# An LSTM step on ScalarE and the reload of output rows: waits, queues and a planner's table

## The chip, the cores and the metric

The kernel runs on one core of one Trainium2 chip. Its engines are TensorE (matrix products; its weight loads are listed apart), VectorE, ScalarE, GpSimd and SyncE, which issues transfers. Time is microseconds on the device. The core takes instructions of each engine in a fixed order; engines wait for each other through semaphores.

## The reference, cut to what matters

A two-layer network: images become tokens (a convolution and an attention), text tokens are joined, layer 0 is a windowed attention and a mixture of eight experts, layer 1 a phasor attention and then an LSTM over 569 time steps of 16 sequences with 256 units. The change lies in the LSTM and in what follows it:

```python
x_proj = jnp.einsum('btd,gd->btg', x, W_ih) + b_ih + b_hh
def step(carry, xp):
    h, c = carry
    gates = xp + h @ W_hh.T
    i, f, g, o = jnp.split(gates, 4, axis=-1)
    c = jax.nn.sigmoid(f) * c + jax.nn.sigmoid(i) * jnp.tanh(g)
    h = jax.nn.sigmoid(o) * jnp.tanh(c)
    return ((h, c), h)
...
inc = jnp.cumsum(w, axis=1)          # w: hidden states that a linear layer selects
prefix = inc - w
suffix = inc[:, -1:, :] - inc
return 2.0 * lstm_out + prefix * fw_att + suffix * bw_att
```

The suffix needs the sum over all steps, so no output row is final before the last step.

## The kernel before, in words

The first half of the time goes to the tokens, the attention of layer 0 and the experts. From about 1,723 us on, two things run side by side: the LSTM's 569 steps, a chain in which each step needs the one before, and the layers' work on later time steps (layer 1's attention and the projections `x_proj`, the functions `fronts` and `backs`), called the other streams here.

*Time blocks.* The steps are cut into ten blocks (`BLOCKS`: 32 steps, eight times 64, 25), a block into units of 8 steps (`STEPS`). The projections of a block are added up by VectorE into `xp` (L1591) and stored to HBM in `XCD` (input, forget and cell gates) and `XOD` (output gate) by SyncE's queue (L1596, L1600). For each unit `load` (L1672) brings them back into `XC` and `XO`, two buffers each, as soon as the block's `backs` are done. So the first step of a block can't begin before the other streams have finished that block.

*A step* (`steps`, L1664). Two PSUM banks hold the sums: `GC` (96 columns, three gates) and `GO` (64 columns, output gate). ScalarE copies the step's input into them (`begin`, L1691, and `begin_out`, L1696), TensorE adds the recurrent products (L1734, L1743), ScalarE reads the sums through tanh (L1754, L1760), and TensorE clears the banks with products with zeros (`clear`, L1684) so that they can be begun again for the next step. VectorE makes the cell state (L1766, L1772) and turns it (L1779), ScalarE takes its tanh (`th`, two buffers in turn, L1787), VectorE turns the output gate (L1792) and writes the hidden state `X` (L1794). Then the next step's recurrent products begin.

*The planner.* The order of each engine's instructions is not left to a scheduler: `Order` lists the pieces of the chain and of the other streams on a clock of its own and puts them down one by one. For the chain it reads the table `STEP` (L129): for every piece the engine, how long that engine is taken, when the result is there, after which piece it comes and with what hop between them. A piece of another stream is put in where it ends before the chain will need its engine, by that table, with a small allowance (`plan.spare`, set at L1713). When the chain can't go on, because a block is not projected yet, the other streams get the engines to themselves until it can. On the chip each engine then works in exactly that order: an instruction that stands ahead of the chain's next one is done first.

*Dependences and waits.* The framework derives the waits from what each instruction reads and writes, those between two instructions of the same engine too. An instruction holds one wait itself; further ones are put into separate semaphore instructions in front of it, on the same engine's queue. A wait for a later instruction of an engine stands for all earlier ones, and the framework leaves out what it thus knows already.

*The output rows.* `sums_of` (L1801) makes the running sums for each run of 16 steps. There is no room for all output rows while the other streams use the memory, so finished ones go to HBM (`PD`, L1868). When the other streams are done, their memory becomes `O` (L1902), the rows are loaded back into it by SyncE's queue in pieces of eight units, 1 MB each (L1905), and later rows are written to it directly. After the last step the suffix is added to `O` and it is stored (L1934, L1938).

Of the kernel before, what the change touches and what calls it, by code (L numbers as in the profile page):

```python
# [12 lines left out]
AF = mybir.ActivationFunctionType  # L13
# [72 lines left out]
def time_of_rows():  # L86
# [44 lines left out]
    "out hidden": ("PE", 0.24, 0.42, "hidden", -0.17),  # L131
    "gates": ("ACT", 0.16, 0.26, "hidden", 0.065),
    "clear": ("PE", 0.06, 0.25, "gates", 0.06),
    "out gate": ("ACT", 0.12, 0.22, "out hidden", 0.065),
    "input": ("ACT", 0.14, 0.24, "clear", 0.065),
    "products": ("DVE+", 0.22, 0.22, "gates", 0.035),
    "cell": ("DVE+", 0.19, 0.19, "products", 0.035),
    "cell turned": ("DVE", 0.13, 0.21, "cell", 0.035),
    "out clear": ("PE", 0.06, 0.25, "out gate", 0.06),
    "tangent": ("ACT", 0.14, 0.23, "cell turned", 0.095),  # L140
    "out input": ("ACT", 0.12, 0.22, "out clear", 0.065),
    "out gate turned": ("DVE", 0.15, 0.23, "out gate", 0.035),
    "state": ("DVE+", 0.18, 0.18, "tangent", 0.035),
}
# [150 lines left out]
def kernel(ctx: ExitStack, tc: tile.TileContext, a: dict, out: bass.AP):  # L295
    nc = tc.nc
# [56 lines left out]
    before = route.tile([128, E, E], F32, name="before")  # L353
    strict = route.tile([128, 128], F32, name="strict")
    ones = route.tile([128, 128], F32, name="ones")
    between = route.tile([128, 1], F32, name="between")
# [18 lines left out]
    first = Order()  # L375
# [1288 lines left out]
    def steps():  # L1664

        act = ls.tile([128, 4 * 32], F32, name="act_init", tag="act", bufs=3)
        nc.vector.memset(act[:, 96:], 0.0)
        before, begun, loaded = None, set(), set()  # L1670

        def load(k):  # L1672
            j, u, n = UNITS_ALL[k]
            loaded.add(k)
            nc.sync.dma_start(
                XC[k % 2][:, :n, :], XCD[j][:, :, u : u + n, :].rearrange("a b t x -> (a b) t x")
            )
            for q in range(4):
                nc.sync.dma_start(XO[k % 2][32 * q + NB : 32 * q + 32, :n, :], XOD[j][q, :, u : u + n, :])
            plan.mark(("loaded", k), 4.0)  # L1680

        def clear(g, n, last):
            for q in range(4):
                nc.tensor.matmul(  # L1684
                    g[32 * q : 32 * q + 32, :n], nil[:, :32], nil[:, :n], start=True, stop=last
                )

        def begin(k, t):
            begun.add((k, t))
            yield "input"  # L1690
            nc.scalar.copy(GC[:, :96], XC[k % 2][:, t, :])  # L1691

        def begin_out(k, t):
            begun.add((k, t, "out"))
            yield "out input"
            nc.scalar.copy(GO[:, :64], XO[k % 2][:, t, :])  # L1696

        def ready(k):

            n = 2 * UNITS_ALL[k][0]  # L1700
            return [("back", n + i, slot) for i in range(2) for slot in range(2)]

        for k, (j, u, n) in enumerate(UNITS_ALL):
            if k not in loaded:
                for event in ready(k):
                    yield "at", event
                load(k)
            yield "at", ("loaded", k)

            after = [("back", 2 * (j + 1) + i, slot) for i in range(2) for slot in range(2)]  # L1710
            done = sum(plan.past(e) for e in after) if j + 1 < len(BLOCKS) else 4
            ahead = plan.past(("back", 2 * j + 3, 0))
            plan.spare = 0.0 if ahead else 0.2 if done >= 4.0 * u / BLOCKS[j][1] - AHEAD else 0.45  # L1713
            if (j, u) in run_of:
                r = run_of[j, u]
                if r >= 4:
                    yield "at", ("sums", r - 4)
                hidden[r] = XS_OF[r % 4][:, :, : RUNS[r][2], :]
            X = hidden[r][:, :, u - RUNS[r][1] :, :]
            for t in range(n):  # L1720
                at, last = f"{k}_{t}", (k, t) == (len(UNITS_ALL) - 1, n - 1)
                if before is None:
                    yield "hidden"
                    clear(GC, 96, True)
                    clear(GO, 64, True)
                if (k, t) not in begun:
                    yield from begin(k, t)
                    yield from begin_out(k, t)
                yield "hidden"
                for kk in range(2 if before is not None else 0):  # L1730
                    for half in range(2):
                        for q in range(4):
                            own = 512 * (q // 2) + 96 * (2 * (q % 2) + half)
                            nc.tensor.matmul(  # L1734
                                GC[32 * q : 32 * q + NB * (1 + half), :96],
                                before[:, kk, NB * (1 - half) :], Whh[:, kk, own : own + 96],
                                start=False, stop=(kk + half == 2),
                            )
                yield "out hidden"
                for kk in range(2 if before is not None else 0):  # L1740
                    for q in range(4):
                        own = 512 * (q // 2) + 384 + 64 * (q % 2)
                        nc.tensor.matmul(  # L1743
                            GO[32 * q : 32 * q + 32, :64], before[:, kk, :],
                            Whh[:, kk, own : own + 64], start=False, stop=(kk == 1),
                        )
                if (
                    k + 1 < len(UNITS_ALL) and k + 1 not in loaded
                    and all(plan.past(e) for e in ready(k + 1))
                ):  # L1750
                    load(k + 1)
                nxt = (k, t + 1) if t + 1 < n else (k + 1, 0)
                yield "gates"
                nc.scalar.activation(act[:, :96], GC[:, :96], AF.Tanh, scale=0.5)  # L1754
                if not last:
                    yield "clear"
                    clear(GC, 96, False)
                to = ls.tile([128, 64], F32, name=f"to{at}", tag="to", bufs=3)
                yield "out gate"
                nc.scalar.activation(to, GO[:, :64], AF.Tanh, scale=0.5)  # L1760
                ahead = nxt[0] in loaded and plan.past(("loaded", nxt[0]))
                if ahead:
                    yield from begin(*nxt)
                ab = ls.tile([128, 2, 32], F32, name=f"ab{at}", tag="ab", bufs=2)
                yield "products"
                nc.vector.scalar_tensor_tensor(  # L1766
                    ab, act[:, :64].rearrange("p (g x) -> p g x", g=2), 1.0,
                    act[:, 64:].rearrange("p (g x) -> p g x", g=2), ALU.add, ALU.mult,
                )
                act = ls.tile([128, 4 * 32], F32, name=f"act{at}", tag="act", bufs=3)  # L1770
                yield "cell"
                nc.vector.scalar_tensor_tensor(  # L1772
                    act[:, 96:], ab[:, 1, :], 0.5, ab[:, 0, :], ALU.mult, ALU.add
                )

                cT = ls.tile([128, 2 * NB], F32, name=f"cT{at}", tag="cT", bufs=2)
                yield "cell turned"
                nc.vector.transpose(cT, act[:, 96:])  # L1779
                if not last:  # L1780
                    yield "out clear"
                    if j >= len(BLOCKS) - 2:
                        product(GO[:, :D], ident, Whh[:, 0, :D], start=True, stop=True)
                    clear(GO, 64, False)
                th = ls.tile([128, 2, NB], F32, name=f"th{at}", tag="th", bufs=2)
                yield "tangent"
                nc.scalar.activation(th.rearrange("p k x -> p (k x)"), cT, AF.Tanh, scale=0.5)  # L1787
                if ahead:
                    yield from begin_out(*nxt)
                toT = ls.tile([128, 2, 2 * NB], F32, name=f"toT{at}", tag="toT", bufs=2)  # L1790
                yield "out gate turned"
                nc.vector.transpose(toT.rearrange("p k x -> p (k x)"), to)  # L1792
                yield "state"
                nc.vector.scalar_tensor_tensor(  # L1794
                    X[:, :, t, NB:], toT[:, :, NB:], 1.0, th, ALU.add, ALU.mult
                )
                before = X[:, :, t, :]
            if u + n == RUNS[r][1] + RUNS[r][2]:
                plan.mark(("steps", r))

# [85 lines left out]
    with tc.manual_schedule(engines=ENGINES):  # L1886
# [13 lines left out]
        bg.close()  # L1900
        op = ctx.enter_context(tc.tile_pool(name="out", bufs=1))
        tail["O"] = op.tile([128, sum(map(len, UNITS_OF)), D], F32, name="O")  # L1902
        for u in range(0, tail["stored"], 8):
            u1 = min(u + 8, tail["stored"])
            nc.sync.dma_start(tail["O"][:, u:u1, :], PD[:, u:u1, :])  # L1905
        plan.run([chain, rest])
    route.release()

# [153 lines left out]
```

## Time and profile before

| | us |
|---|---|
| median of 5 runs | 3381.17 (3378.01 to 3384.28) |
| the profiled execution, its own time | 3380.79 |
| its span, first to last instruction | 3378.9 |
| tokens, attention, experts: up to the first step | 1,723 |
| the 569 steps | 1,723 to 3,338.6 |
| of them with other streams' work beside | 1,723 to about 3,167 |
| suffix and stores after the last step | 3,338.6 to 3,378.9 |

Busy time of the engines in three stretches, from the profile's view by windows:

| window, us | TensorE | VectorE | ScalarE | GpSimd |
|---|---|---|---|---|
| 2400 to 2600 | 192.93 | 147.14 | 111.76 | 21.65 |
| 3200 to 3300 | 80.28 | 52.12 | 45.16 | 0.00 |
| 3300 to 3379 | 33.77 | 46.45 | 18.03 | 0.00 |

How to read the profile. A time line row has the start, the time taken, the engine (PE is TensorE, PEld its weight loads, DVE VectorE, ACT ScalarE, SP SyncE; a q behind it means that the engine's queue works and not the engine), the line, the operation, what it writes and reads, and in brackets how long the engine had been idle and what ended that. The chain of work lists start, duration and piece. A view of one line gives the number of its instructions, their shortest, median and longest duration in ns, and the first and last start. Ends of products on TensorE are modelled.

### The profile page before, as it was taken

The page shows a single profiled execution, that of the slowest core. Times are in us where ns is not written, and L with a number is a line of the kernel's source. Part 1 is how long each engine was busy: PE and PEld are TensorE (multiplying, and loading weights), DVE is VectorE, ACT ScalarE, POOL GpSimd, SP SyncE. Part 2 cuts the span into 40 slices and gives each one's busy share as a digit, 9 for nine tenths or more (in the row PEclk, how much of TensorE's full clock was granted, in tenths as well). Part 3 has the DMA queues.
Part 4 walks back from the last instruction along what each step waited for, and adds up shares of the span by engine and source line. Part 5 has one row for each costly group of instructions (what it writes and reads, how often), then busy time and mean ns, then how long its engine had stood idle before and what let it go on. Part 6 is the DMA issues. An engine that isn't in the chain of part 4 may idle for free.

```text
span 3378.9 us, 135926 instructions
## 1 busy us (share of the span) xinstructions
PE 3069.7 (91%) x57536; PEld 2228.4 (66%) x57536; DVE 2016.0 (60%) x6785; ACT 1483.0 (44%) x5032; POOL 789.7 (23%) x1524
## 2 busy tenths in 40 slices
PE   6999989999859999997899999999999999999884
PEld 3666666666648888886565666666666666666553
DVE  4677777766732222222565777777777777776555
ACT  3545545454412222221444456555555555554442
POOL 1243554455433332222311010011111000100000
PEclk8999999999969999999999999999999999999997
DMA  5111221111166666664333333333333333333413
GB/s 178 52 44 59 86 82 49 56 39 42 35 238 232 224 228 225 234 225 144 97 101 82 94 77 81 82 97 86 90 82 88 92 83 84 79 94 79 143 34 119
DMA packets 272627, 366.39 MB, mean 108 GB/s; under 512 B 144096, under 2 KB 219792, under 8 KB 258960
## 3 DMA queue, kind: packets, MB, share of 16 engines
q1 hardware_dynamic: 250368, 308.51, 30.9%
q0 software_dynamic: 14496, 39.75, 3.1%
q8 instruction: 451, 7.39, 0.9%
q10 hardware_dynamic: 7152, 9.43, 0.9%
q14 instruction: 160, 1.31, 0.1%
HBM read 239.07 MB, written 118.49 MB: 106 GB/s over the span
## 4 chain that ended last, share of the span: by engine, by line
PE 40%; DVE 5%; ACT 3%; DMA 2%; issue 2%; SPq 1%; POOL 0%; ACTq 0%; DVEq 0%; POOLq 0%
PE gates L1734 12%; PE xm_False L1085 6%; PE out_gate L1743 3%; PE po_False L1085 2%; PE ek L1085 2%; PE v L1085 2%; PE z L1085 2%; PE eq L1085 2%; PE r_False L1085 2%; PE ds_False L1085 1%; PE out_gate L1684 1%; ACT act L1754 1%; PE gates L1684 1%; PE fin L1085 1%; DVE ab L1766 1%
## 5 line engine op out<-in xcount | busy, mean ns | idle before, releaser
L1734 PE MATMUL gates<-W_hh,X 128*16 128x96 f32 (+1 forms) x18176 | 490.0, 248 | 47.3 <-DVE X L1794 40.8
L1734 PEld LDWEIGHTS gates<-W_hh,X 128*16 128x16 f32 (+1 forms) x18176 | 379.9, 103 | 223.5 <-DVE X L1794 194.8
L1754 ACT ACTIVATE act<-gates 128x96 f32<-128x96 f32 x568 | 141.7, 249 | 462.0 <-PE gates L1734 454.5
L1248 ACT ACTIVATE hT<-hp,w 128x256 f32<-128x256 f32 x316 | 132.3, 471 | 480.9 <-PE hp L1241 304.3
L1766 DVE SCALAR_TENSOR_TENSOR ab<-act 128x64 f32<-128x64 f32 x568 | 128.0, 225 | 303.3 <-ACT act L1754 296.7
L1085 PE MATMUL xm_False<-W_ih,dxT_False 128*32 128x256 f32 x4352 | 293.0, 380 | 7.0 <-DVE xp_False L1591 4.9
L1255 PE MATMUL y<-w,hT 128*128 128x256 f32 x1264 | 289.7, 382 | 5.2 <-ACT hT L1248 1.5
L1241 PE MATMUL hp<-xt,w 128*128 128x256 f32 x1264 | 287.9, 381 | 1.0 <-ACT hT L1248 1.0
L1684 PEld LDWEIGHTS <-nil 128*32 128x32 bf16 x4552 | 177.5, 94 | 147.7 <-issue 54.2
L1255 PEld LDWEIGHTS y<-w,hT 128*128 128x128 f32 x1264 | 236.8, 190 | 45.2 <-ACT hT L1248 14.3
L1241 PEld LDWEIGHTS hp<-xt,w 128*128 128x128 f32 x1264 | 240.2, 191 | 35.7 <-ACT hT L1248 1.4
L1184 POOL DMA_INDIRECT YT<-ys,to x158 | 153.3, 970 | 439.5 <-DVE ys L1261 407.9
L1261 DVE TENSOR_TENSOR ys<-y,w 128x512 f32<-128x512 f32 x79 | 54.6, 692 | 316.5 <-PE y L1255 218.2
L1743 PE MATMUL out_gate<-W_hh,X 128*32 128x64 f32 x9088 | 235.5, 220 | 4.8 <-ACT out_gate L1696 3.4
L1691 ACT COPY gates<-xc 128x96 f32<-128x96 f32 x569 | 138.4, 243 | 173.0 <-PE gates L1684 105.5
L1743 PEld LDWEIGHTS out_gate<-W_hh,X 128*32 128x32 f32 x9088 | 188.5, 110 | 8.6 <-ACT out_gate L1696 3.6
L693 PE MATMUL wqk<-wxT,wqkv 128*128 128x128 f32 x1152 | 153.2, 281 | 7.6 <-ACT wxT L687 7.3
L908 POOL DMA_INDIRECT XS<-XN,at x144 | 148.5, 1031 | 45.6 <-issue 24.7
L693 PEld LDWEIGHTS wqk<-wxT,wqkv 128*128 128x128 f32 x1152 | 142.0, 194 | 24.4 <-ACT wxT L687 12.5
L1794 DVE SCALAR_TENSOR_TENSOR X<-toT,th 128x32 f32<-128x32 f32 x569 | 107.5, 189 | 78.1 <-ACT th L1787 72.7
L1787 ACT ACTIVATE th<-cT 128x32 f32<-128x32 f32 x569 | 130.2, 229 | 50.9 <-DVE cT L1779 7.4
L1298 POOL TENSOR_SCALAR r_False_rstd<-r_False_mv,cols 128x2 f32<-128x2 f32 x36 | 15.7, 436 | 583.0 <-DVE r_False_mv L1293 583.0
(356 smaller groups left out, 6511.7 us busy)
## 6 DMA issues: line engine op xcount, KB each, us to landing
w<-in_wpack SPq DMA_DIRECT2D x79, 1154.0 KB
taps<-in_taps SPq DMA_DIRECT2D x16, 1764.0 KB
xc<-XCD SPq DMA_DIRECT2D x71, 384.0 KB
XCD<-xp_False SPq DMA_DIRECT2D x256, 96.0 KB
xs<-XS SPq DMA_DIRECT2D x79, 258.0 KB
yg<-YT SPq DMA_DIRECT2D x72, 256.0 KB
HD<-h SPq DMA_DIRECT2D x72, 128.0 KB
fh<-HD SPq DMA_DIRECT2D x72, 128.0 KB
```

What stands on the lines that cost most here:

```text
L693: nc.tensor.matmul(qk[:, j, m, :], wqkv[:, k, D * j + 128 * m : D * j + 128 * m + 128], xT[:, k, :], start=(k == 0), stop=(k == 1),)
L908: fill(0, nc.gpsimd.indirect_dma_start(out=XS[0], out_offset=bass.IndirectOffsetOnAxis(ap=at[:, i, c - lo : c - lo + 1], axis=0), in_=XN[p ...
L1085: nc.tensor.matmul(out[own], lhsT[:, own], rhs, start=start, stop=stop)
L1184: keep(nc.gpsimd.indirect_dma_start(out=YT, out_offset=bass.IndirectOffsetOnAxis(ap=to[:, i : i + 1], axis=0), in_=ys[:, i, :], in_offset= ...
L1241: nc.tensor.matmul(hp[:, i, :], w1[:, k, hc * 128 : (hc + 1) * 128], xT[:, k, :], start=(k == 0), stop=(k == 1),)
L1255: nc.tensor.matmul(y[:, i, :], hT[:, hc, 128 * i : 128 * i + 128], w2[:, hc, :], start=(hc == 0), stop=(hc == 3),)
L1684: nc.tensor.matmul(g[32 * q : 32 * q + 32, :n], nil[:, :32], nil[:, :n], start=True, stop=last)
L1691: nc.scalar.copy(GC[:, :96], XC[k % 2][:, t, :])
L1734: nc.tensor.matmul(GC[32 * q : 32 * q + NB * (1 + half), :96], before[:, kk, NB * (1 - half) :], Whh[:, kk, own : own + 96], start=False, ...
L1743: nc.tensor.matmul(GO[32 * q : 32 * q + 32, :64], before[:, kk, :], Whh[:, kk, own : own + 64], start=False, stop=(kk == 1),)
L1754: nc.scalar.activation(act[:, :96], GC[:, :96], AF.Tanh, scale=0.5)
L1766: nc.vector.scalar_tensor_tensor(ab, act[:, :64].rearrange("p (g x) -> p g x", g=2), 1.0, act[:, 64:].rearrange("p (g x) -> p g x", g=2), ...
```

## The change

Four parts, in the order of the diff:

- In `STEP`, the times for which ScalarE is taken by the out gate's tanh, the input's copy, the tangent and the out input's copy are each 0.04 us longer, and the tangent's hop after the turned cell is 0.04 in place of 0.095 us.
- `begin`, `begin_out` and the two tanh of the sums keep their instructions (`begun`, `read`), and `ordered_by_products` declares to the framework that there is no dependence between a bank's copy and its tanh, and between the tanh and the next copy. Between any two of them stands a product or a clearing on TensorE that waits for the first and is waited for by the second.
- After the hidden state of a step, while there is a list `tail["reload"]`, one piece of two units (256 KB) of the output rows is reloaded, by ScalarE's queue.
- In place of the loads in pieces of eight units by SyncE's queue, that list is made.

```diff
-    "out gate": ("ACT", 0.12, 0.22, "out hidden", 0.065),
-    "input": ("ACT", 0.14, 0.24, "clear", 0.065),
+    "out gate": ("ACT", 0.16, 0.22, "out hidden", 0.065),
+    "input": ("ACT", 0.18, 0.24, "clear", 0.065),
...
-    "tangent": ("ACT", 0.14, 0.23, "cell turned", 0.095),
-    "out input": ("ACT", 0.12, 0.22, "out clear", 0.065),
+    "tangent": ("ACT", 0.18, 0.23, "cell turned", 0.04),
+    "out input": ("ACT", 0.16, 0.22, "out clear", 0.065),
...
-        before, begun, loaded = None, set(), set()
+        before, begun, loaded, read = None, {}, set(), {}
...
         def begin(k, t):
-            begun.add((k, t))
             yield "input"
-            nc.scalar.copy(GC[:, :96], XC[k % 2][:, t, :])
+            begun[k, t] = nc.scalar.copy(GC[:, :96], XC[k % 2][:, t, :])
+            ordered_by_products(begun[k, t], read.pop(0, None))

         def begin_out(k, t):
-            begun.add((k, t, "out"))
             yield "out input"
-            nc.scalar.copy(GO[:, :64], XO[k % 2][:, t, :])
+            begun[k, t, 1] = nc.scalar.copy(GO[:, :64], XO[k % 2][:, t, :])
+            ordered_by_products(begun[k, t, 1], read.pop(1, None))
+
+        def ordered_by_products(ins, other):
+            if other is not None and before is not None:
+                tc.declare_no_dep(
+                    ins.ins, other.ins, reason="a product between them waits for the first"
+                )
+            return ins
...
                 yield "gates"
-                nc.scalar.activation(act[:, :96], GC[:, :96], AF.Tanh, scale=0.5)
+                read[0] = ordered_by_products(
+                    nc.scalar.activation(act[:, :96], GC[:, :96], AF.Tanh, scale=0.5), begun.pop((k, t))
+                )
...
                 yield "out gate"
-                nc.scalar.activation(to, GO[:, :64], AF.Tanh, scale=0.5)
+                read[1] = ordered_by_products(
+                    nc.scalar.activation(to, GO[:, :64], AF.Tanh, scale=0.5), begun.pop((k, t, 1))
+                )
...
                 before = X[:, :, t, :]
+                if tail.get("reload"):
+                    part = tail["reload"].pop(0)
+                    nc.scalar.dma_start(tail["O"][:, part, :], PD[:, part, :])
...
-        for u in range(0, tail["stored"], 8):
-            u1 = min(u + 8, tail["stored"])
-            nc.sync.dma_start(tail["O"][:, u:u1, :], PD[:, u:u1, :])
+        tail["reload"] = [slice(u, min(u + 2, tail["stored"])) for u in range(0, tail["stored"], 2)]
         plan.run([chain, rest])
+        assert not tail["reload"]
```

## The prediction

> **What bounds the kernel now.** I read the busy times, then one step of the recurrence in the time line, then who waits for whom around the block ends and the reload. In a step with nothing between its parts the time line is a closed chain:
>
> ```profile
> 3281.03 0.19 DVE L1794 SCALAR_TENSOR_TENSOR X<-toT,th 128x32 f32<-128x32 f32 x1 [0.17 <-ACT th L1787]
> ...
> 3281.27 0.85 PE L1734 MATMUL gates<-W_hh,X 128*16 128x96 f32 x32 [0.35 <-DVE X L1794]
> ...
> 3282.25 0.25 ACT L1754 ACTIVATE act<-gates 128x96 f32<-128x96 f32 x1 [0.99 <-PE gates L1734]
> ...
> 3282.53 0.22 DVE L1766 SCALAR_TENSOR_TENSOR ab<-act 128x64 f32<-128x64 f32 x1 [0.68 <-ACT act L1754]
> ...
> 3282.79 0.19 DVE L1772 SCALAR_TENSOR_TENSOR act<-ab 128x32 f32<-128x32 f32 x1
> ...
> 3283.02 0.21 DVE L1779 STREAM_TRANSPOSE cT<-act 128x32 f32<-128x32 f32 x1
> ...
> 3283.26 0.23 ACT L1787 ACTIVATE th<-cT 128x32 f32<-128x32 f32 x1
> 3283.53 0.19 DVE L1794 SCALAR_TENSOR_TENSOR X<-toT,th 128x32 f32<-128x32 f32 x1 [0.17 <-ACT th L1787]
> ```
>
> From X to X is 2.50 us. The 568 intervals between the starts of L1794 take 1,613 us, so 193 us lie above 568 x 2.50. I sorted them: 110.2 us at the seven block ends (last step of a block, numbers 31, 95, ... 415), 70.7 us spread over the other steps up to 504, 11.1 us after that, 1.3 in the first. The first kind, at step 415:
>
> ```profile
> 2920.43 0.23 ACT L1787 ACTIVATE th<-cT 128x32 f32<-128x32 f32 x1 [0.92 <-DVE cT L1779]
> 2931.50 0.24 ACT L1691 COPY gates<-xc 128x96 f32<-128x96 f32 x1 [10.84 <-DMA xc<-XCD]
> ```
>
> The chain of work there, in order of time, shows what runs meanwhile: TensorE works through other streams' products, which stand ahead of the next recurrent product in its queue, and these end later (2933.21) than the input's copy:
>
> ```profile
> 2931.05 0.86 PE r_False L1085 x16
> 2931.91 0.43 PE ds_False L1085 x8
> 2932.34 0.86 PE z L1085 x16
> 2933.21 0.66 PE gates L1734 x32
> ```
>
> The third kind follows the reload of the output rows on SyncE's queue (first the issues, then on ScalarE the copy that waits 5.45 us for a load queued behind them):
>
> ```profile
> 3167.72 5.49 SPq L1905 DMA_DIRECT2D O<-PD  x8
> ```
> ```profile
> 3193.59 0.22 ACT L1696 COPY out_gate<-xo 128x64 f32<-128x64 f32 x1 [5.45 <-DMA xo<-XOD]
> ```
>
> **The change, part by part.** (1) *ScalarE's own waits.* A wait for two engines puts a separate semaphore instruction in front. Views of the two lines show who has one:
>
> ```profile
> L1754 ACTq EVENT_SEMAPHORE  x568: 17/17/17, 1727.7 to 3337.2; - x190
> ```
> ```profile
> L1787 ACT ACTIVATE th<-cT x569: 213/229/233, 1725.0 to 3338.3; 128x32 f32<-128x32 f32 x190
> ```
>
> L1754 has it at every step, L1787 never. From the trace's semaphore events, an instruction of ScalarE whose late wait sits in that separate instruction starts 83 ns after the semaphore rises (median of 993 waits for TensorE); with the wait in itself it starts after 24 ns (342 waits for TensorE, 143 for VectorE). So the separate instruction costs 59 ns where it holds the late wait.
> The order of the changed kernel's instructions shows that the gates' tanh, the out gate's tanh and both copies lose it. But with those waits gone nothing on ScalarE tells the tangent any more that its buffer of two steps ago was written, so the tangent gets a wait for ScalarE beside the one for VectorE, in 566 of 569 steps, and the separate instruction holds the late one, VectorE's. That form stands 25 times in the trace of before, mostly at L589: 84 ns. On the chain: gates -59 ns, tangent +60 ns, sum 0. The waits for ScalarE itself are met long before (ten instructions or more back), so they cost nothing. The out gate's tanh and the copies also start 59 ns sooner, but they are no part of the chain above: the out gate's result is turned before the tangent ends, and the copies end over 1 us before the next products. Taken: 0. Bounds: -33 us (gates' 59 ns x 568, the tangent's free) to +34 (the reverse).
>
> (2) *The planner's table.* ScalarE's four entries are occupied 0.04 us longer, and the tangent is planned 0.055 us sooner. Nothing is computed differently, but the planner fits less of the other streams' work into a step. I counted, in both orders, the columns of other streams' products between one recurrent product and the next:
>
> | last step of block | columns before | us above 2.50 | columns after |
> |---|---|---|---|
> | 31 | 116,480 | 62.35 | 125,056 |
> | 95 | 6,144 | 0.45 | 26,880 |
> | 159 | 30,208 | 12.58 | 40,704 |
> | 223 | 11,264 | 2.56 | 32,512 |
> | 287 | 25,088 | 11.76 | 32,512 |
> | 351 | 20,864 | 8.46 | 32,512 |
> | 415 | 29,568 | 12.07 | 32,512 |
>
> What is not done inside the steps is left at the end of the block, where the chain stands still behind it. Price: 12.58/30,208 = 0.416 ns a column at 159, 0.408 at 415, 0.405 at 351, 0.469 at 287. At 0.416 the six ends from 95 on take 82.2 us, now 47.9: +34.3. Step 31 pays 0.535 a column: 8,576 more, +4.6. Together +39, from +34 (0.40 a column) to +49 (0.469).
>
> The steps themselves get lighter: in the full blocks from 96 to 415 some 3,130 columns a step become 2,950 to 3,000. Steps up to 3,072 columns already run at 2.51 (median), so little comes back. The block from 416 (2,536 columns a step) has 0.079 us a step above 2.50, those five 0.145; on that line 2,950 gives 0.124, or 9 us over some 440 steps. Columns above 3,072 in a step fall by 34,800: at 0.416 that is 14.5 us. Taken: -12. Bounds: 0, and -31 (all 497 steps at 0.079 in place of 70.7 us).
>
> (3) *The reload.* Gone are 8 issues on SyncE's queue, 7.5 MB at some 400 GB/s. They cost steps 507, 508, 509, 511 and 512: 1.94 + 0.63 + 0.58 + 4.58 + 2.59 = 10.3 us above 2.50 (xo late, TensorE without instructions for 1.6 us, clock granted at 0.63 to 0.84). New are 31 issues of 256 KB on ScalarE's queue, one a step from 508 on, behind the copy to the out gate and before the gates' tanh. The nearest rows: 0.34 to 0.44 us for O<-PD on SyncE, 0.55 at least for 256 KB out<-O on ScalarE, 1.16 in the median with the queues full. The copy starts 0.02 to 0.30 us after X, the tanh 1.22 after X, so 0.55 is hidden by the recurrent product; 256 KB in 2.50 us is 105 GB/s, so queues are not full. At 1.16 it would be some 0.3 late, 31 times: 9 us. Taken 0.
> The first of them waits for the last eight stores of the projections (the output rows take their memory), on ScalarE, with the tanh, and so the whole chain, behind it. Those stores follow an addition on VectorE one step earlier: 0.9 us, eight issues of 0.38 on SyncE (3163.49 to 3166.43 now), and 1.6 at most to land: 5.2 us after X of 507. The issue adds 0.55, and the tanh was due at 3.7: some 2 us late (0 to 4.6). Sum of the part: -8.
> The rows need not come fast: 31 steps and the 30 behind them last 150 us, and the output rows are read only after the last.
> The Trainium skill, DMA: Bandwidth & Descriptors, section Bandwidth, asks for transfers of at least 1 MiB and shows 64 KB at 32% of the peak rate, which speaks against pieces of 256 KB; no run here shows its sizes. By that page's fit for another kind of queue (section Anatomy of one DMA, 2.0 us plus bytes over 436 GB/s) a piece would take 2.6 us, an estimate, and 31 of them one by one 81 us, so that the sum would be the same by the page as by the rows.
>
> **Sum.** 0 + 39 - 12 - 8 = +19 us. The profiled execution took 3380.79 us around a span of 3378.9; the median of the runs is 3381.17, 0.4 more. Predicted: 3400 us.
>
> **Rivals.** *A: the tangent's extra instruction is free, or its wait is met otherwise.* For it: the planner's 0.04 for the tangent is what the trace shows now (turn ends 3283.23, tangent 3283.26). Against it: the 25 rows at 84 ns. Then -33 us: 3367, faster than before. It decides once the tangent starts within about 50 ns of its turn, since the table's cost must be beaten.
> *B: a column saved in a step is worth as much as one at the block's end.* For it: TensorE is busy for 193 of 200 us in the middle of the steps. Against it: steps of 3,072 columns run at the chain's pace. Then the steps return -31, the body comes to +8, and the reload's -8 cancels it: 3381, no change.
> *C: the issues on ScalarE hold the tanh.* +9 for 31 issues, +3 for a longer first wait: 3412. For it: the 1.16 us rows; against: these are of full queues.
>
> **Chances.** Forecast, with C beside it: 0.64. B 0.20, A 0.16. A measurement of this kernel can tell 0.2% (6.8 us) from no change. Below -6.8 lies A and a little of B, within lies B: faster 0.16, same 0.20, slower 0.64. The range takes the bounds of the block ends and of the steps, and B: 3376 to 3419.
>
> **What would show it.** Right: L1754 without, L1787 with a semaphore instruction at each step; X to X still 2.50 in empty steps; block ends of 13 to 14 us four times over, 11 at step 95 where there was none; no step above 5 us after 505 and TensorE's clock whole there. Wrong: empty steps of 2.44 (A); block ends as long, but fewer steps above 2.55 (B); steps of 2.8 from 508 to 539 (C).

## The result, and the profile after

The changed kernel takes 3377.41 us (median of 27 runs, 3373.66 to 3388.33) where the kernel before took 3380.60 in 49 runs beside them: ratio 0.9994, 95% interval 0.9989 to 0.9999. That is no change by the bound of 0.2%. The forecast was 3400, slower. The profiled execution of the changed kernel has a span of 3379.4 us (3378.9 before); it took 3381.27 us itself, 3.9 above the median of its kernel, so that the traces differ by +0.5 where the medians differ by -3.2.

The starts of `X` (L1805 now, L1794 before) cut both spans into the same pieces. "Above" means the sum over steps of what a step takes beyond 2.50 us. The steps are split at 497 here, because the end of the other streams moves between 503 and 507 in the runs below.

| us | before | after | difference |
|---|---|---|---|
| up to the first `X` | 1725.3 | 1726.6 | +1.4 |
| above, steps 0 to 496 without the block ends | 69.8 | 48.0 | -21.8 |
| above, block end at step 31 | 62.4 | 55.1 | -7.3 |
| above, the six block ends from 95 on | 47.9 | 81.1 | +33.2 |
| above, steps 497 to 567 | 13.2 | 6.0 | -7.3 |
| after the last `X` | 40.4 | 42.7 | +2.3 |
| sum | | | +0.5 |

The first row is nothing of the change: both kernels do the same there, and it lay between 1712.5 and 1729.4 in the profiles of this study. Two profiled executions with one order of steps also differ by up to 4.4 us in the second row (before and e3 below). Chips differ too (before: 3371 or 3380 us), so times are compared with those of before on the same chip.

A step with nothing in it, in the time line of the changed kernel (start, duration, engine, line, operation):

```profile
3286.63 0.19 DVE L1805 SCALAR_TENSOR_TENSOR X<-toT,th 128x32 f32<-128x32 f32 x1 [0.23 <-ACT th L1798]
...
3286.88 0.85 PE L1741 MATMUL gates<-W_hh,X 128*16 128x96 f32 x32 [0.42 <-DVE X L1805]
...
3287.80 0.25 ACT L1762 ACTIVATE act<-gates 128x96 f32<-128x96 f32 x1 [1.05 <-PE gates L1741]
...
3288.57 0.21 DVE L1790 STREAM_TRANSPOSE cT<-act 128x32 f32<-128x32 f32 x1
...
3288.87 0.23 ACT L1798 ACTIVATE th<-cT 128x32 f32<-128x32 f32 x1 [0.26 <-DVE cT L1790]
...
3289.14 0.19 DVE L1805 SCALAR_TENSOR_TENSOR X<-toT,th 128x32 f32<-128x32 f32 x1 [0.23 <-ACT th L1798]
```

From product to tanh it is 0.92 us where it was 0.98; from the turn's start to the tangent 0.30 where it was 0.24 (3283.02 to 3283.26). X to X is 2.51. The wait has moved, as the view of the tangent's line shows (instruction, count, shortest/median/longest ns, first to last start); L1762 has no such line any more:

```profile
L1798 ACT ACTIVATE th<-cT x569: 212/229/238, 1726.4 to 3336.5; 128x32 f32<-128x32 f32 x190
L1798 ACTq EVENT_SEMAPHORE  x566: 17/17/17, 1732.6 to 3336.4; - x189
```

Block ends, in ScalarE's time line: at step 95, where the kernel before had 0.45 us above an empty step, and at step 415:

```profile
2039.12 0.24 ACT L1690 COPY gates<-xc 128x96 f32<-128x96 f32 x1 [7.25 <-DMA xc<-XCD]
...
2937.46 0.24 ACT L1690 COPY gates<-xc 128x96 f32<-128x96 f32 x1 [10.33 <-DMA xc<-XCD]
```

The chain of work behind the second shows what then still stands ahead on TensorE:

```profile
2938.57 1.07 PE z L1085 x16
2939.65 0.70 PE gates L1741 x32
```

So the ends became longer as forecast. What paid for them lies in the steps. One place of it, in VectorE's time line of the kernel before, between the turned out gate and `X`:

```profile
2242.31 0.21 DVE L1779 STREAM_TRANSPOSE cT<-act 128x32 f32<-128x32 f32 x1
2242.44 0.20 DVE L1792 STREAM_TRANSPOSE toT<-to 128x64 f32<-128x64 f32 x1
2242.57 0.38 DVE L1290 BATCH_NORM_STATS2 f_st<-fh 128x6 f32<-128x256 f32 x1
2242.88 0.17 DVE L1794 SCALAR_TENSOR_TENSOR X<-toT,th 128x32 f32<-128x32 f32 x1
```

The tangent starts at 2242.55 there, and `X` 0.33 after it, not 0.26: VectorE is still at another stream's statistics, and `X` doesn't wait for the tangent but for its own engine. The same stretch after:

```profile
2241.80 0.21 DVE L1790 STREAM_TRANSPOSE cT<-act 128x32 f32<-128x32 f32 x1
2241.93 0.20 DVE L1803 STREAM_TRANSPOSE toT<-to 128x64 f32<-128x64 f32 x1
2242.36 0.19 DVE L1805 SCALAR_TENSOR_TENSOR X<-toT,th 128x32 f32<-128x32 f32 x1 [0.23 <-ACT th L1798]
```

In steps 1 to 496 `X` came over 0.30 us after the tangent's start 126 times before and 6 times after (30 times with the table alone, e1 below; the rest of the fall is the tangent's later start). Counted in the two orders, one of another stream's longer pieces (statistics, a tensor-scalar or a scalar-tensor-tensor) stands directly before `X` at 131 of the 569 steps before, at 40 after.

The reload, in the changed kernel's time line of SyncE's and ScalarE's queues: the last of eight stores of the projections, then the copy to the out gate, the first piece and the tanh behind it.

```profile
3181.59 0.34 SPq L1600 DMA_DIRECT2D XOD<-xp_True  x1
```
```profile
3180.17 0.22 ACT L1695 COPY out_gate<-xo 128x64 f32<-128x64 f32 x1
3183.40 0.35 ACTq L1811 DMA_DIRECT2D O<-PD  x1
3183.80 0.25 ACT L1762 ACTIVATE act<-gates 128x96 f32<-128x96 f32 x1 [3.42 <-DMA XOD<-xp_True]
```

ScalarE stands still for 3.42 us, until the stores have landed. Steps 507 and 508 take 4.88 and 3.13; behind them none is above 2.77.

### The profile page after: what moved, and what is told of

It reads as the page before. It is cut to its first block, busy times and chain, and to the rows that moved or that the text cites. A ratio compares the mean times of both kernels' runs of the same rounds, so it can differ in the third digit from the quotient of the medians.

```text
span 3379.4 us, 134328 instructions
## 1 busy us (share of the span) xinstructions
PE 3070.4 (91%) x57536; PEld 2240.0 (66%) x57536; DVE 2032.2 (60%) x6787; ACT 1472.0 (44%) x5030; POOL 786.6 (23%) x1524
## 4 chain that ended last, share of the span: by engine, by line
PE 38%; DVE 7%; ACT 5%; issue 2%; DMA 1%; POOL 0%; SPq 0%; ACTq 0%; DVEq 0%; POOLq 0%
PE gates L1741 13%; PE xm_False L1085 6%; PE out_gate L1750 2%; PE ek L1085 2%; PE po_False L1085 2%; PE z L1085 2%; PE eq L1085 2%; PE v L1085 1%; PE ds_False L1085 1%; ACT act L1762 1%; PE r_False L1085 1%; ACT th L1798 1%; DVE ab L1777 1%; DVE cT L1790 1%; DVE act L1783 1%
## 5 line engine op out<-in xcount | busy, mean ns | idle before, releaser
L1741 PE MATMUL gates<-W_hh,X 128*32 128x96 f32 (+1 forms) x18176 | 489.4, 248 | 64.0 <-DVE X L1805 61.2
L1741 PEld LDWEIGHTS gates<-W_hh,X 128*32 128x32 f32 (+1 forms) x18176 | 374.8, 103 | 258.3 <-DVE X L1805 243.7
L1762 ACT ACTIVATE act<-gates 128x96 f32<-128x96 f32 x568 | 142.1, 250 | 449.4 <-PE gates L1741 442.3
L1241 PEld LDWEIGHTS hp<-xt,w 128*128 128x128 f32 x1264 | 240.1, 191 | 35.6 <-ACT hT L1248 1.5
L1684 PEld LDWEIGHTS <-nil 128*32 128x32 bf16 x4552 | 189.4, 94 | 111.8 <-issue 53.5
L1805 DVE SCALAR_TENSOR_TENSOR X<-toT,th 128x32 f32<-128x32 f32 x569 | 110.3, 194 | 121.9 <-ACT th L1798 118.1
L1301 POOL TENSOR_SCALAR d_False_rstd<-d_False_mv 128x2 f32<-128x2 f32 (+1 forms) x36 | 9.0, 249 | 675.6 <-DVE d_False_mv L1293 550.8
L908 POOL DMA_INDIRECT XS<-XN,at x144 | 148.4, 1031 | 45.6 <-issue 24.7
```

Source lines behind the costliest of these rows:

```text
L908: fill(0, nc.gpsimd.indirect_dma_start(out=XS[0], out_offset=bass.IndirectOffsetOnAxis(ap=at[:, i, c - lo : c - lo + 1], axis=0), in_=XN[p ...
L1241: nc.tensor.matmul(hp[:, i, :], w1[:, k, hc * 128 : (hc + 1) * 128], xT[:, k, :], start=(k == 0), stop=(k == 1),)
L1684: nc.tensor.matmul(g[32 * q : 32 * q + 32, :n], nil[:, :32], nil[:, :n], start=True, stop=last)
L1741: nc.tensor.matmul(GC[32 * q : 32 * q + NB * (1 + half), :96], before[:, kk, NB * (1 - half) :], Whh[:, kk, own : own + 96], start=False, ...
```

## The experiments

Two theories stood after this. T: the parts add up as the prediction has them, and only the sizes of two terms (the lighter steps, the end at step 31) are off. R: the waits or the reload brought far more than was forecast, and the table's loss is what the sum had. Each part was tried alone first.

**The table alone.** Before, with the four entries of `STEP` and nothing else:

```diff
-    "out gate": ("ACT", 0.12, 0.22, ...     -    "tangent": ("ACT", 0.14, 0.23, "cell turned", 0.095),
+    "out gate": ("ACT", 0.16, 0.22, ...     +    "tangent": ("ACT", 0.18, 0.23, "cell turned", 0.04),
```

> The kernel before with the planner's table of the change alone; its TensorE order has the same columns at the block ends as the changed kernel (125,056 at step 31, 26,880, 40,704, four times 32,512). Theory T (the table moves other streams' work to the block ends, +33 us there, and the lighter steps give it back, -22; step 31 comes out 7 us shorter): all of this is seen here without the removed waits, so some +4 us against before (0 to +8), steps above 2.50 us by some 48 us in all, block ends 11.0, 16.6 and four times 13.4 us. Rival R (the removed waits, not the lighter steps, gave the -22 in the steps and the -7 at step 31): the table alone costs its block ends, +30 to +35 us, and the steps stay at 70 us above 2.50. In both, the gates' tanh comes 0.981 us after the products' start and the tangent 0.246 us after the turn's.

3384.26 us against 3380.02, ratio 1.0014 (1.0004 to 1.0024). The ends are those of the changed kernel (55.9, then 81.8 in six), and the steps 1 to 496 fall by 24.2 us by themselves. The end at 31 is the table's doing too. So R's loss of 30 to 35 us is not there, and the waits and the reload can't have brought that much.

**The waits alone.** Before, with `ordered_by_products` and the old table and reload:

```diff
+                read[0] = ordered_by_products(
+                    nc.scalar.activation(act[:, :96], GC[:, :96], AF.Tanh, scale=0.5), begun.pop((k, t))
```

> The kernel before with the undeclared dependences alone (table and reload as before; the columns at the block ends are those of before). Theory T: the gates' tanh 0.921 us after the products' start (0.981 before), the tangent 0.306 after the turn's (0.246), empty steps 2.50 to 2.51, time within 3 us of before. Rival R: steps above 2.50 fall from 71 to some 48 us and step 31 loses 7 us, so -25 to -30 us.

3370.60 us, ratio 0.9973 (0.9964 to 0.9983), -9.4: neither T's 3 nor R's 25. Product to tanh falls by 61 ns in the median and turn to tangent rises by 60, as in the changed kernel, and the empty step stays at 2.50; but steps 1 to 496 lose 11 us. The reason is in the segments below.

**The reload alone.** Before, with the list of pieces issued by ScalarE:

```diff
+                if tail.get("reload"):
+                    part = tail["reload"].pop(0)
+                    nc.scalar.dma_start(tail["O"][:, part, :], PD[:, part, :])
```

> The kernel before with the reload alone, 256 KB a step by ScalarE's queue. Theory T: steps from 505 on lose the 10 us of the slow ones and gain one stop of 2 to 3 us before the first issue, then some 2 us are lost after the last step (the last sums and the waits for the pieces on VectorE): -4 to -7 us. Rival (the issues hold the gates' tanh, which the changed kernel hides by its earlier start of 59 ns): steps of 2.6 us or more while the pieces are issued, so -3 us or nothing. Everything up to step 500 as before.

3371.51 us, ratio 0.9980 (0.9971 to 0.9989), -8.5, more than the 4 to 7 that were expected. In the trace the steps from 497 on give 5.6 us; the steps before them have the order of the kernel before, and what they give (4.4 in steps 0 to 496, 1.4 at step 31) has no cause in the edit. The 31 issues cost nothing that shows: behind the first two the steps are 2.50, a few 2.6 to 2.9 as before. The first piece holds ScalarE (3.38 us before the tanh), here at step 503, since with the old table the projections end four steps sooner; steps 503 and 504 take 4.88 and 4.23.

**The waits and the reload together**, that is the changed kernel with the old table (the diff of e1 in reverse).

> The kernel after with the planner's table of before: waits and reload as in after. Theory (parts add up): -9.4 (e2) - 8.5 (e3) = -18 us against before, some 3362; block ends 110 us, steps 59, after step 505 some 2 us, no stop where the reload begins. Then the table costs some 15 us inside the changed kernel. Rival (the gains of waits and reload overlap, as the changed kernel's 3 us in all suggest): -9 to -12 us, and the table costs under 9.

3353.80 us against 3371.17 on the same chip, ratio 0.9943 (0.9929 to 0.9956): -17.4. These two add up (9.4 + 8.5 = 17.9). The stop where the reload begins is there too, which was not expected (steps 503 and 504 take 4.87 and 3.59). With the table put on top the ratio is 0.9994, so the table that costs 4.2 us alone costs some 17 here (0.0051 of 3377). What is lost shows when the steps' surplus is cut by engine. In steps 1 to 496, sums over each segment's own median (so the 60 ns of the two waits are not in them), from the starts in the traces, good to about 1 us (e7 and e8 are the two halves of the table, below):

| us | before | e1 table | e2 waits | e6 waits, reload | after | e7 | e8 |
|---|---|---|---|---|---|---|---|
| `X` to recurrent product to tanh (TensorE's other work) | 45.6 | 35.6 | 42.6 | 44.2 | 37.5 | 35.8 | 43.2 |
| tanh to `X` (VectorE, ScalarE) | 21.0 | 6.8 | 13.1 | 13.6 | 6.5 | 18.7 | 12.5 |
| `X` over 0.30 after the tangent, times | 126 | 30 | 15 | 15 | 6 | 108 | 24 |
| steps 497 to 567, above 2.50 | 13.2 | 6.6 | 10.6 | 5.8 | 6.0 | 9.7 | 9.5 |

In the second row the table takes 14.2, the waits take 7.9, and both together 14.5. They take the same microseconds. Where VectorE is late for `X` anyway, the tangent's extra 60 ns are hidden behind it, so the gates' 59 ns are a net gain in those steps; the table plans `X` sooner and moves VectorE's piece elsewhere, and then the 60 ns are on the chain again. The last row has the second such pair: the table by itself takes 6.6 of the reload's harm (the burst meets three steps of 3.4 to 3.7 in place of five of 3.1 to 7.1), the small pieces by themselves 5.6, both 7.2. What the parts thus take twice is 7.6 us in the second row and 5.0 in the last, most of the 13 by which the table is dearer here than alone.

**The table by halves**: the four occupancies (e7), or the tangent's hop (e8).

> Before with the four longer occupancies alone (not the tangent's earlier start). The order has 130,688 columns less than nothing but ends and steps shifted: at the ends from step 95 on 178,688 columns (before 123,136), in the other steps 72,704 fewer, those above 3,072 in a step 22,272 fewer. Theory U (a column taken out of a step is worth the same in every step, 24.5 us / 87,296 columns = 0.28 ns from e1): the steps' excess falls by 20 us, to 50. Theory V (only columns above 3,072 a step count, 24.5 / 34,816 = 0.70 ns from e1): it falls by 15.7, to 55. The ends from 95 on take 74 us at 0.416 ns a column by both.

> Before with the tangent planned 0.055 us sooner alone. At the ends from step 95 on 214,016 columns (before 123,136), in the other steps 103,552 fewer, those above 3,072 in a step 26,752 fewer. Theory U (0.28 ns for every column taken out of the steps): the steps' excess falls by 29 us, to 42. Theory V (0.70 ns for those above 3,072 alone): it falls by 18.8, to 52. The ends from 95 on take 89 us at 0.416 ns a column by both.

One profiled run each: 3379.67 and 3394.16 us beside a median of 3371.17 before. The six ends take 69.7 and 89.9 us (74 and 89 expected). The steps fall by 12.4 and 11.5: neither U nor V, and e8, which takes more columns out of the steps, doesn't gain more. The occupancies take 9.8 us from TensorE's segments and 2.3 from the others; the hop takes 2.4 and 8.5. The gain in the steps is two things, and the count of columns measures neither: e8 takes out more of them than e7 and gains a quarter as much in TensorE's segments. What decides TensorE's part was not found.

**The tangent's new wait taken away.** `act`, `to` and `th` get fixed buffers used in turn, and the framework is told that a buffer's next writer needs no wait for its last one, as VectorE has read it in between. This is put on the changed kernel (e4) and on the changed kernel with the old table (e5):

```diff
-                th = ls.tile([128, 2, NB], F32, name=f"th{at}", tag="th", bufs=2)
+                th = ths[no % 2]
...
-                nc.scalar.activation(th.rearrange("p k x -> p (k x)"), cT, AF.Tanh, scale=0.5)
+                alone(nc.scalar.activation(th.rearrange("p k x -> p (k x)"), cT, AF.Tanh, scale=0.5), "th", 2)
```

> The changed kernel with buffers of their own for the gates, the out gate and the tangent, taken in turn, and no dependence declared between two writes of one buffer, since VectorE has read it in between: the tangent waits for VectorE alone and has no separate semaphore instruction. Order of all engines as in the changed kernel. Theory T (the 59 ns that the gates' tanh won were paid back by the tangent): the tangent 0.246 us after the turn, empty steps 2.44 to 2.45 in place of 2.506, the last 60 steps 3.5 us shorter, and of the other 500 those that run at the chain's pace too, some 20 us faster than the changed kernel (4 to 33). Rival (the tangent is not on the chain, or the separate instruction costs nothing): no more than 2 us.

> The kernel after with the same fixed buffers for gates, out gate and tangent as in e4, and with the planner's table of before. Theory (the parts add up): against before, the waits alone were worth -9.4 us (e2), the reload alone -8.5 (e3), the tangent's freed wait -25.7 (e4 against after), sum -44 us: some 3336; block ends as long as before (110 us above 2.50), 20 us less than 58.8 in the steps, 2.445 us in empty steps. Rival (with the old table the steps carry more of the other streams' columns, so TensorE sets a good part of them and a shorter chain helps only the rest): the steps' excess stays near 59, the tangent's freed wait is worth half, and the sum is -31 us: some 3349, no better than e4's 3352.

e4: 3351.73 us, ratio 0.9928 (0.9914 to 0.9941), 25.7 below the changed kernel's median (22 by the two ratios). e5: 3336.53 against 3371.17, ratio 0.9901 (0.9885 to 0.9916); a second set of runs below gave 0.9915. Both beat both kernels. The tangent's line in e5 has no semaphore instruction, and in an empty step it starts 0.24 after the turn's start again, X to X 2.44:

```profile
L1815 ACT ACTIVATE th<-cT x569: 213/229/258, 1713.4 to 3291.2; 128x32 f32<-128x32 f32 x190
```
```profile
3276.74 0.19 DVE L1824 SCALAR_TENSOR_TENSOR X<-toT,th 128x32 f32<-128x32 f32 x1 [0.17 <-ACT th L1815]
...
3278.68 0.21 DVE L1806 STREAM_TRANSPOSE cT<-act 128x32 f32<-128x32 f32 x1
...
3278.92 0.23 ACT L1815 ACTIVATE th<-cT 128x32 f32<-128x32 f32 x1 [0.20 <-DVE cT L1806]
...
3279.18 0.19 DVE L1824 SCALAR_TENSOR_TENSOR X<-toT,th 128x32 f32<-128x32 f32 x1 [0.17 <-ACT th L1815]
```

With the old table the freed wait is worth 17.3 us (e5 against e6, same chip; 14 by the ratios), not 25.7. From the first to the last `X` the profiles differ by 18.4 us here and by 30.6 between after and e4. `X` is late for VectorE in 131 steps again, and the steps 1 to 496 keep 44.5 us above 2.50 where e4 has 19.1. So e5 is 34.6 us below before (29.8 in the second set), as its rival had it (31), and not 44. By the ratios it is 4 to 9 us better than e4: with the tangent freed, the table costs about as little as it did alone.

**The reload's first stop.** e5 once more, e5 with the first piece four steps later, and e5 with the pieces issued by SyncE:

```diff
+                if tail.get("reload") and tail["off"]:
+                    tail["off"] -= 1
-                if tail.get("reload"):
+                elif tail.get("reload"):
```
```diff
-                    nc.scalar.dma_start(tail["O"][:, part, :], PD[:, part, :])
+                    nc.sync.dma_start(tail["O"][:, part, :], PD[:, part, :])
```

> e5 once more, as the base for the next two: ratio 0.990 to before as in the first run; steps 503 and 504 last 5.0 and 4.1 us (4.2 us above two empty steps) because the first piece of the reload waits on ScalarE for the last stores of the projections.

> e5 with the first piece of the reload issued four steps later, still by ScalarE. Theory (the stop is the wait for the projections' last eight stores, which have landed by then): steps 503 and 504 last 2.45 to 2.8, no later step is longer for it, 4 us less than e5. Rival (the stop belongs to the first large load itself, or to other work at the end of the projections): it comes four steps later, or stays; no gain.

> e5 with the pieces of 256 KB, one a step, issued by SyncE in place of ScalarE. Theory (it is the pieces' size and pace that cost nothing, whichever queue issues them; the wait for the stores then stands in SyncE's queue, where nothing of the step waits): no stop at 503 and 504, 4 us less than e5, no step of over 3 us behind it. Rival (SyncE's queue is the trouble: loads of gate inputs queue behind the pieces or behind the wait, as behind the 1 MB pieces of before): a load comes late, one or more steps of 3 to 7 us after 503, as long as e5 or longer.

Against 3370.87 on their chip: e5 3341.12, ratio 0.9915 (0.9901 to 0.9928); e10 3336.25, 0.9895 (0.9880 to 0.9910); e9 3337.47, 0.9904 (0.9888 to 0.9919). The times can't tell the three apart. The steps can: 503 and 504 take 4.84 and 4.11 in e5, 2.45 and 2.86 in e10, 2.44 and 2.87 in e9, and steps 497 to 567 are 2.6, -1.0 and 0.3 above 2.50. ScalarE's time line of e10 at the place where e5 stood:

```profile
3133.54 0.22 ACT L1707 COPY out_gate<-xo 128x64 f32<-128x64 f32 x1
3134.74 0.25 ACT L1776 ACTIVATE act<-gates 128x96 f32<-128x96 f32 x1 [0.99 <-PE gates L1755]
```

So the stop was the wait for the stores in front of the tanh, some 4 us, and not the piece. In the second of the two steps TensorE's clock is lower: in the second profile of e5 it is granted at 0.52 from 3131.0 to 3133.5 us, behind the stop, and the recurrent product takes 1.42 us in place of 0.85; in e10 it stays at 1.00 there. In e9, with the pieces on SyncE's queue, one step reaches 3.23 (517) and none 4. So it is not the queue; the size and the pace of the pieces were changed together, and no run takes the two apart.

## Why the prediction was wrong

The forecast was +19 us, and the trace has +0.5. The step that failed is part (2): it priced all that the table moves by TensorE's columns. That held for the six later block ends. It failed at step 31, which the prediction had at +4.6 and which came to -7.3, and in the steps, which it had at -12 and which came to -21.8.

- *Chain (0): right.* The gates' 59 ns are gained, the tangent's 60 lost, by the mechanism named. From semaphore to start it is 83 ns now for ScalarE's late waits for VectorE in a separate instruction (192 waits, most of them the tangent's) and 23 for its waits for TensorE (1,140).
- *The six ends from 95 on (+34.3): right.* Measured +33.2; 0.416 ns a column gave 11.2, 16.9 and four times 13.5, and the trace has 11.0, 16.6 and four times 13.4.
- *Step 31 (+4.6): wrong, -7.3, the largest miss.* The prediction priced its 8,576 more columns at 0.535 ns. The end isn't set by columns alone: 116,480 of them took 62.4 us before, 125,056 took 55.1 after. Between the two starts of `X` TensorE was busy for 55.9 us and idle for 9.0 before, busy for 54.8 and idle for 2.8 after. Its time line has four waits of over 0.7 us there before, for other streams' work on ScalarE and VectorE:

```profile
1818.67 0.64 PE L1085 MATMUL r_False<-V,w_False 128*32 128x256 f32 x8 [2.15 <-ACT kT L1275]
...
1828.36 1.07 PE L1085 MATMUL ds_False<-V,kT 128*32 128x256 f32 x16 [2.58 <-DVE S L1468]
...
1831.41 0.85 PE L1085 MATMUL xm_False<-W_ih,dxT_False 128*32 128x256 f32 x12 [1.39 <-ACT dxT_False L1275]
...
1859.01 1.93 PE L1085 MATMUL xm_False<-W_ih,dxT_False 128*32 128x256 f32 x32 [2.04 <-DVE xp_False L1591]
```

and one after it:

```profile
1826.01 1.93 PE L1085 MATMUL xm_False<-W_ih,dxT_False 128*32 128x256 f32 x32 [1.23 <-DVE dxT_False L1271]
```

TensorE's idle time there is 7.2 to 9.0 us in the eight profiles with the old table and 2.8 to 3.5 in the three with the new one. So the 0.535 ns had some 9 us of waits in it that are no matter of columns, and the order that the new table makes has fewer of them. Why TensorE is not busy for longer with more columns stays open; its clock was granted at 0.97 in this stretch before and at 1.00 after.
- *Lighter steps (-12, bounds 0 to -31): the mechanism that failed.* It held that the steps below 3,072 columns "already run at 2.51", so little comes back, and priced TensorE's columns alone. TensorE's segments did fall by two thirds of that (8.1 us; 10.0 in e1). What was left out is the second engine that the planner fills: VectorE's and ScalarE's part of a step fell by 14.5 (21.0 to 6.5). In all -21.8 by the split used here, -22.4 up to step 504. The sentence in part (1) that the out gate's result "is turned before the tangent ends" was right, but it didn't ask what VectorE does between that turn and `X`.
- *Reload (-8): about right.* -7.3, with the first stop as described (some 2 us late was forecast; steps 507 and 508 were 2.4 and 0.6 over; the prediction's own 0.9, 2.9 and 1.6 add up to 5.4 and not 5.2, and its 0.34 to 0.44 us an issue are the shortest and the median of a row whose longest is 1.60). But it isn't a part by itself: the table alone already brings 6.6 of it.
- *After the last step: +2.3, not foreseen.* It comes with the table's occupancies: 43.2 after the last `X` in e1 and e7, 42.9 in e4, and 40.0 to 41.5 in all runs without them. How they do it was not followed.

The 18.5 us that were missed are step 31 (11.9), the lighter steps (9.8) and the six ends (1.1), less the 2.3 after the last step, 1.4 before the first and 0.7 of the reload. The time is rival B's, 3381, but not by its reason, and so by luck: B had 31 us come back from the steps by TensorE's columns, where 21.8 came back, most of it on VectorE and ScalarE, and step 31 made up the rest. (The top of the stated range, by the bounds that it names, is 3422 and not 3419.) Rival C's late issues were not there. Rival A's tangent was not free; freed in e4 it brings 22 to 26 of A's 33 us.

On the page that was weighed against the reload: the Trainium skill, DMA: Bandwidth & Descriptors, section Bandwidth, asks to batch transfers to at least 1 MiB for three quarters of the peak rate. The kernel before moves pieces of that size, at some 400 GB/s; the changed one gave the rate up and lost nothing by it, since the rate doesn't limit this stage: 256 KB a step is hidden (e10), while the burst of 1 MB pieces, with loads of the next units queued behind it, cost 10.3 us in the kernel before and 3.1 in e1.

## What to carry to other kernels

When a planner's table changes, count what it moves on every engine it fills, not on the busiest one alone: TensorE's columns told the six later block ends to about 1 us in the changed kernel and in e8 and to 4 in e7, failed at step 31, and VectorE's pieces held more of the steps than they did. Two edits that each remove waiting from the same stretch don't add; ask of each gain what other part of the change would remove it too. And a wait taken from one instruction may come back in front of another: here a step with nothing in it gained nothing from the first until the second was freed as well (2.50, then 2.44 us; e5 is 1% below before).

## What the runs showed of the hardware

On ScalarE a wait in a separate semaphore instruction cost 59 to 60 ns when it was the late one (83 ns from semaphore to start, against 23 or 24). It cost nothing where the separate instruction held an early wait: `X` on VectorE has one in front of it at each step and starts 23 ns after the tangent's semaphore (514 waits after the change):

```profile
L1805 DVEq EVENT_SEMAPHORE  x569: 21/21/21, 1726.5 to 3336.6; - x190
```

On ScalarE itself the copy of the gates' input has one at 64 steps after the change, and starts 23 ns after the late wait for TensorE that it holds itself (57 of them). The Trainium skill, Perfetto Trace Analysis, section Identifying Dependency Chains, says that instructions waiting on several engines may get such instructions in front of them; here an instruction with a second wait on its own engine gets one too, and which of its waits lands in it decides the price.

An issue of 256 KB on ScalarE's queue once a step took 0.33 to 0.35 us and was not to be seen in the step's time, though ScalarE is on the chain: 31 of them, each beside the recurrent product. Only the first showed, by its wait for the stores.
